# Two graph layers with top-p attention: other slots for logits, exponentials and search passes in step 2, and another order of the closing work on VectorE

## The chip, the cores and the metric

The kernel runs on one core of one Trainium2 chip. The metric is the device time of one execution in microseconds (us); smaller is better. A profiled execution shows what each engine does: TensorE (PE in the profile, with its weight loads as PEld), VectorE (DVE), ScalarE (ACT), GpSimd (POOL) and SyncE (SP, which here only issues DMAs).

## The reference, cut to what matters

There are N = 2708 nodes with D = 256 features. A first layer gives x1 from `adj @ x`. The second layer runs two steps; R below is the row-normalized `adj + I`.

```python
for n in range(2):
    q = Xa @ W1.T @ W2.T;  k = Xa @ W3.T
    probs = softmax(q @ k.T)               # (N, N)
    mask = smallest set of largest probs that reaches 0.9 per row
    A = probs * mask / sum
    Xf = R @ Xf;  Xa = A @ Xa
    Z = Z + Xf @ U1[n].T + Xa @ U2[n].T
h = X + Z
x = layernorm(X + layernorm(h) * g + b)    # two normalizations per row at the end
```

## The kernel before

All matrices are cut into tiles of 128 rows: NB = 22 tiles, of which the last, called EDGE, has 20 rows. The work order is written by hand. An engine executes its instructions in the order in which the program emits them[...], so the place in the program text is the place in each engine's queue.

**Step 2** is the loop `for per in range(NB + 1)`. Each turn is a period, and a period has six groups, g = 0 to 5 (NG = 6). Four tiles are in flight in a period:

- Tile per + 2 (`b_exp`) gets its logits, in three pieces of up to 1024 columns, into one PSUM buffer (`ps_lg`, bufs=1). The PE makes a piece at L506. ScalarE takes the exponential of each piece (`exps2`, L818), and after the first piece also a half-power exponential (L822). The first piece of the tile of the next period is made at g = 5 already. Its row maximum is taken by VectorE in `shift` (L815).
- Tile per + 1 (`b_act`) gets two trials of a threshold on ScalarE in `try_act`, k = 0 and 1: a Relu pass (L922), a Sign pass (L925), and small operations that end in b.u[k] (L936; L938 for k = 1).
- Tile per (`b_dve`) is finished on VectorE: `last_level` (L959 to L962, which needs b.u[1] of the period before), then `finish2`, whose parts are spread over the groups: a masking pass (L976), 20 maxima (L979), sorting (L576, L578), selection among ties (L989 to L1007), and the final mask (L1010). After it comes `begin_search` of tile per + 2 at g = 5 (L826 to L829), which needs all three exponentials.
- Tile per - 1 (`t_mul`) is multiplied on the PE. In each group `turn` makes four transposes (L526, into the PSUM tile tr with two buffers), ScalarE copies them to SBUF (wT, L529), and `products` makes the product one group later (L563).

`r_units` puts the sparse product with R between these on the PE (L730). Its operands are gathered by GpSimd DMAs (L698, yg), and VectorE takes the result in `r_out` (L753 in periods 0 to 10, L768 from period 11). From period 11 finished rows also appear, and `final_slot` normalizes them in stages: at g = 2 it loads x1b, at g = 3 VectorE makes the statistics of up to four tiles (L1037, L1038), at g = 5 ScalarE takes the square roots (L1087), and at g = 0 of the next period VectorE makes reciprocals (L1089, L1090), ScalarE normalizes (L1047) and GpSimd applies g and b (L1062, L1063); at g = 1 finished tiles are stored (L1070). A tile goes through this twice, since there are two normalizations.

In a group the emission order is: on the PE `turn`, then logits, then `r_units`, then `products`; on ScalarE the wT copy, then the exponentials, then the trial passes.

**The closing work** follows the loop. In the last period (per = 22) the EDGE tile's 20 rows are multiplied in one go by `edge_product` (L543, L545, L549), in four row groups which `edge_sum` adds up (a ScalarE copy L240 and a matmul L242). Then come the flags (L1184 to L1197: do the rows stay inside the fast path's assumptions), the arrival of the EDGE tile's sum (L768), and rounds of `final_slot` until all tiles are stored. While the list `tail` is empty, `norm` and `middle` of class Final run on ScalarE and GpSimd; once it isn't, on VectorE (L1045, L1054, L1056).

Of the kernel before, what the change touches and what calls it, by code (L numbers as in the profile page):

```python
# [9 lines left out]
FP = mybir.dt.float32  # L10
I32 = mybir.dt.int32
AF = mybir.ActivationFunctionType
ALU = mybir.AluOpType
# [7 lines left out]
P = 128  # L21
# [127 lines left out]
def fast_path(ctx, tc, c, flags, fint, xT_d, x_d, w0_d, b0_d, w1_d, w2_d, w3_d, u1_d, u2_d, g_d, b_d):  # L149
    nc = tc.nc  # L150
    N, D, DA, NB, DC, KH, CHS, rows = c.N, c.D, c.DA, c.NB, c.DC, c.KH, c.CHS, c.rows
# [8 lines left out]
    small = ctx.enter_context(tc.tile_pool(name="small", bufs=4))  # L160
# [8 lines left out]
    def ps_acc(t=None):  # L169
        acc = ps.tile([P, CH], FP, tag="acc", name="acc")  # L170
        if t == NB - 1:
            nc.vector.memset(acc[:, :D + 1], 0.0)
        return acc

    def ps_misc():
        return ps.tile([P, CH], FP, tag="misc", name="misc")
# [53 lines left out]
    EDGE = NB - 1  # L230
# [5 lines left out]
    def edge_sum(acc, n, stop=True):  # L236

        p = rows(EDGE)
        four = work.tile([P, 4, P], FP, tag="wT", name="four").rearrange("p k i -> p (k i)")
        nc.scalar.copy(four[:, :n], acc[:, :n])  # L240
        whole = ps_acc()
        nc.tensor.matmul(whole[:p, :n], lhsT=fold[:, :p], rhs=four[:, :n], start=True, stop=stop)  # L242
        return whole
# [254 lines left out]
    def logits(s, t, i):  # L498


        p = rows(t)
        lg = ps_lg()
        cs = CHS[2 * i:2 * i + 2]
        for h, (a, b) in enumerate(cs):
            o = slice(DA * h, DA * h + DA)
            nc.tensor.matmul(lg[:p, h, :b - a], lhsT=q[o, t * P:t * P + p], rhs=keys[s][o, i, :b - a],  # L506
                             start=True, stop=True)
        a, b = cs[0][0], cs[-1][1]
        return lg.rearrange("p h n -> p (h n)")[:p, :b - a], a, b
# [7 lines left out]
    NG = (NB + 3) // 4  # L517
# [81 lines left out]
    def exps1(t):  # L599

        p = rows(t)
        e = es[t % 4]
        nmax, srt = st1[t]
        z = small.tile([P, 2], FP, tag="z1", name="z1", bufs=3)
        st1[t] = (srt, z)
        h = 11 * P

        def part(i):
            if i == 0:
                nc.scalar.activation(srt[:p], srt[:p], AF.Exp, bias=nmax[:p], scale=1.0)  # L610
            a, b = ((0, h), (h, N))[i]
            nc.scalar.activation(e[:p, a:b], e[:p, a:b], AF.Exp, bias=nmax[:p], scale=1.0,
                                 accum_out=z[:p, i:i + 1])
        return part
# [76 lines left out]
    later = [[], []]  # L691
    ready = []
# [46 lines left out]
    def za_load(m):  # L739


        if loads.get(m):
            loads[m] = 2
            return None
        loads[m] = 1
        base = work.tile([P, D], FP, tag="in", name="base", bufs=3)
        nc.sync.dma_start(out=base[:rows(m)], in_=za_d[m * P:m * P + rows(m), :])
        return base
# [33 lines left out]
    def e2(t):  # L782
        return es[(t + 2) % 4]
# [30 lines left out]
    def shift(b, lg):  # L814
        nc.vector.tensor_reduce(b.nmax, lg[:, :P], AX.X, ALU.max, negate=True)  # L815

    def exps2(b, i, lg, a, c_):
        nc.scalar.activation(e2(b.t)[:b.p, a:c_], lg, AF.Exp, bias=b.nmax, scale=1.0,  # L818
                             accum_out=b.all[:b.p, i:i + 1])
        if i == 0:  # L820
            nc.scalar.activation(b.half, b.nmax, AF.Identity, bias=part_of[:b.p], scale=0.5)
            nc.scalar.activation(e2(b.t)[:b.p, HC:2 * HC], lg, AF.Exp, bias=b.half, scale=0.5, accum_out=b.roots)  # L822
# [23 lines left out]
    part = exps1(0)  # L846
# [5 lines left out]
    part = exps1(1)  # L852
# [11 lines left out]
    for t in range(NB):  # L864
        acc = ps_acc(t)
        part = exps1(t + 2) if t + 2 < NB else None
        b = None
        if t >= NB - 3:
            b = blocks[t - (NB - 3)] = Block(t - (NB - 3))
        ra_next = finish1(t + 1) if t + 1 < NB else None  # L870
        for g in range(NG):
# [5 lines left out]
            if b and g in (0, 2):  # L877
                lg = logits(1, b.t, g // 2)
# [136 lines left out]
    new, finals, done = [], [], []  # L1015
    tail = []

    mvs = small.tile([P, 4, 2], FP, tag="mvs", name="mvs", bufs=1)
    sds = small.tile([P, 4], FP, tag="sds", name="sds", bufs=1)
    nbs = small.tile([P, 4], FP, tag="nbs", name="nbs", bufs=1)  # L1020
    nc.gpsimd.memset(mvs, 1.0)

    class Final:
# [44 lines left out]
        def store(self):  # L1068
            t, p = self.t, self.p
            nc.sync.dma_start(out=out_d[t * P:t * P + p, :], in_=self.h[:p])  # L1070

    def final_slot(i):


        if i == 2:
            while ready and len(new) < 2:
                new.append(Final(*ready.pop(0)))
                new[-1].load()
        if i == 1:
            while done:  # L1080
                done.pop().store()
        n = len(new) + len(finals)
        if i == 3:
            for k, f in enumerate(new + finals):
                f.stats(k)
        if i == 5 and n:
            nc.scalar.activation(sds[:, :n], mvs[:, :n, 1], AF.Sqrt, bias=c.eps, scale=1.0)  # L1087
        if i == 0 and n:
            nc.vector.reciprocal(sds[:, :n], sds[:, :n])  # L1089
            nc.vector.scalar_tensor_tensor(nbs[:, :n], mvs[:, :n, 0], -1.0, sds[:, :n], op0=ALU.mult, op1=ALU.mult)  # L1090
            for f in finals:
                f.end()
            for f in new:
                f.middle()
            done[:] = finals
            finals[:] = new
            new.clear()

    accs = {}
# [18 lines left out]
    lg = logits(1, 3, 0)  # L1118
    r_units(first - 9)
    try_act(b0, 1, 0)  # L1120
    next_level(b0, 1)
    for per in range(NB + 1):
        n_r = units.get(per, 0)
        b_act = blocks.get(per + 1)
        b_dve = blocks.get(per)
        t_mul = per - 1 if per else None
        if per:
            accs[t_mul] = ps_acc(t_mul)
        masks = None
        b_exp = None  # L1130
        if per and per + 2 < NB:
            b_exp = blocks[per + 2] = Block(per + 2)
        for g in range(NG):
            n = n_r * (g + 1) // NG - n_r * g // NG
            now = later.pop(0)
            later.append([])
            if g == 0:
                if b_exp:
                    shift(b_exp, lg[0])
                r_units(n)  # L1140
            if t_mul == EDGE:
                if g == 0:
                    products(0)
                    edge_product(ya, accs[EDGE], e2(EDGE))
            elif per:
                turn(t_mul, g, ya, accs[t_mul], e2(t_mul))
            if b_exp and g == 3:
                lg = logits(1, b_exp.t, 2)
            if g == NG - 1 and 3 < per + 3 < NB:
                lg = logits(1, per + 3, 0)  # L1150
            if g:
                r_units(n)
            if b_exp and g == 1:
                lg = logits(1, b_exp.t, 1)
            if t_mul != EDGE:
                products(1 if per else 0)
            if b_exp and g in (0, 1, 3):
                exps2(b_exp, (g + 1) // 2, *lg)
            if b_act:
                for k, part in {0: ((0, 0),), 1: ((0, 1), (0, 2), (0, 3)), 2: ((1, 0),), 3: ((1, 1), (1, 2), (1, 3))}.get(g, ()):  # L1160
                    try_act(b_act, k, part)
            if g == 0:
                if b_dve:
                    last_level(b_dve)
                    masks = finish2(b_dve)
                    next(masks)
                final_slot(0)
                if per > 1:

                    t = t_mul - 1  # L1170
                    base = za_load(t)
                    later[0].append(lambda t=t, base=base: arrive(t, base, accs.pop(t), ras.pop(t)[:rows(t)]))
            elif masks:
                next(masks, None)
                if b_exp and g == 5:
                    begin_search(b_exp)
            for f in now:
                f()
            if g:
                final_slot(g)  # L1180
    tail.append(True)


    nc.vector.tensor_scalar(flags[:, 2 * NB:3 * NB], bulk[:, 0, :], 1.0e30, None, op0=ALU.is_ge)  # L1184
# [5 lines left out]
                                   op0=ALU.mult, op1=ALU.is_lt)  # L1190
    nc.vector.tensor_reduce(flags[:, 5 * NB:6 * NB], bulk[:, 5:, :].rearrange("p w t -> p t w"), AX.X, ALU.max)
    nc.vector.tensor_scalar(flags[:, 5 * NB:6 * NB], flags[:, 5 * NB:6 * NB], 8.0, None, op0=ALU.is_ge)
    nc.vector.tensor_reduce(fcol, flags, AX.X, ALU.add)
    accs[EDGE] = edge_sum(accs[EDGE], D)
    pf = ps_misc()
    nc.tensor.matmul(pf[:1, :1], lhsT=fcol, rhs=onec, start=True, stop=True)
    nc.vector.tensor_copy(fint, pf[:1, :1])  # L1197
    t = NB - 1
    base = za_load(t)
    for f in later[0] + later[1]:  # L1200
        f()
    final_slot(0)
    final_slot(1)
    arrive(t, base, accs.pop(t), ras.pop(t)[:rows(t)])
    while ready or finals:
        for g in (2, 3, 5, 0, 1):
            final_slot(g)
    assert not r_queue and len(arrived) == NB

def general_path(ctx, tc, c):  # L1210
# [358 lines left out]
```

## Time and profile before

| | us |
|---|---|
| runs shown, median of 3 | 1396.02 (1394.66 to 1401.23) |
| the profiled execution's own time | 1395.44 |
| its span, first to last instruction | 1393.4 |
| step 2 from period 0's masking pass to the last period | 800.3 to about 1370 |
| one period, periods 2 to 10 | 24.3 to 24.9 |
| one period, periods 16 to 19 | 26.5 to 26.8 |
| last period and closing work | 1370 to 1393.4 |

The own time is 2.0 us above the span, and the median of the runs is 0.6 us above the own time. A period is read as the distance between two starts of L976, which occurs once in each. In step 2 VectorE is busy for nearly the whole period; the PE and ScalarE have pauses in it, and which of the pauses count is the question of the prediction.

### The profile page before, as it was taken

How to read it: one execution, taken by the hardware profiler on the slowest of the kernel's cores; microseconds unless marked ns; L12 is line 12 of the kernel's file. 1: busy time of each engine (PE TensorE's matmuls, PEld its weight loads, DVE VectorE, ACT ScalarE, POOL GpSimd, SP SyncE). 2: the span in 40 equal slices, each digit the busy share in tenths (PEclk: the TensorE clock that was granted, in tenths of full speed). 3: DMA queues.
4: the chain of work that ended last, by engine and by line, in shares of the span. 5: the costliest groups of instructions: out<-in, count | busy, mean ns of one | idle time of the engine just before them, and what ended most of it. 6: DMA issues, size and time to landing. Idle time of an engine off the chain costs nothing.

```text
span 1393.4 us, 18921 instructions
## 1 busy us (share of the span) xinstructions
PE 1279.4 (92%) x5788; PEld 898.7 (64%) x5788; DVE 1044.1 (75%) x3482; ACT 743.9 (53%) x1340; POOL 645.0 (46%) x595
## 2 busy tenths in 40 slices
PE   8999999988999999999998849999998988898884
PEld 6877877833567666666666437777665766566662
DVE  2544545865888887776751379999999988999996
ACT  1000000035455555555554438888887887899951
POOL 1000000014544532775555286776734757677870
PEclk9999999999999999999999879999999999999997
DMA  6544544512222110232223245545432544345351
GB/s 184 179 152 151 164 147 150 165 36 66 67 91 65 52 56 9 88 101 63 65 64 94 84 132 156 159 146 156 138 98 88 158 137 128 114 147 177 123 146 36
DMA packets 92830, 157.94 MB, mean 113 GB/s; under 512 B 16356, under 2 KB 65196, under 8 KB 92720
## 3 DMA queue, kind: packets, MB, share of 16 engines
q1 hardware_dynamic: 66434, 100.59, 22.7%
q0 software_dynamic: 20544, 51.17, 13.1%
q10 hardware_dynamic: 5742, 4.89, 1.3%
q8 instruction: 48, 0.79, 0.2%
q14 instruction: 62, 0.51, 0.1%
HBM read 125.33 MB, written 31.26 MB: 112 GB/s over the span
## 4 chain that ended last, share of the span: by engine, by line
PE 55%; DVE 36%; issue 3%; ACT 3%; another core or an unknown queue 1%; POOL 1%; DMA 0%; ACTq 0%; DVEq 0%; POOLq 0%
PE acc L563 16%; PE acc L255 15%; PE lg L506 6%; DVE cand L979 6%; DVE w L1007 5%; PE tr L526 5%; DVE e L1010 4%; DVE w L976 4%; PE misc L677 3%; DVE srt L576 3%; DVE spare L578 3%; PE acc L649 2%; PE misc L427 2%; PE acc L461 2%; PE misc L422 2%
## 5 line engine op out<-in xcount | busy, mean ns | idle before, releaser
L529 ACT COPY wT<-tr 128x512 f32<-128x512 f32 (+2 forms) x258 | 131.9, 518 | 242.0 <-PE tr L526 158.6
L563 PE MATMUL acc<-ya,wT 128*128 128x256 f32 (+1 forms) x924 | 235.8, 396 | 12.3 <-ACT wT L529 8.8
L563 PE MATMUL acc<-x,wT 128*128 128x256 f32 (+1 forms) x924 | 233.0, 391 | 6.6 <-ACT wT L529 6.6
L698 POOL DMA_INDIRECT yg<-yf_d,ix x154 | 192.6, 1251 | 95.3 <-PE misc L730 50.2
L698 POOL DMA_INDIRECT yg<-v_d,ix x154 | 194.8, 1265 | 85.5 <-PE tr L526 35.2
L563 PEld LDWEIGHTS acc<-x,wT 128*128 128x128 f32 (+1 forms) x924 | 166.5, 191 | 88.0 <-issue 48.5
L563 PEld LDWEIGHTS acc<-ya,wT 128*128 128x128 f32 (+1 forms) x924 | 172.2, 194 | 67.9 <-issue 26.4
L255 PE MATMUL acc<-y,adj_t 128*128 128x257 f32 (+1 forms) x924 | 208.8, 382 | 0.0
L365 POOL DMA_INDIRECT adj_t<-in_adj,ix x154 | 171.8, 1116 | 50.8 <-issue 39.9
L255 PEld LDWEIGHTS acc<-y,adj_t 128*128 128x128 f32 (+1 forms) x924 | 171.7, 189 | 33.8 <-issue 10.2
L730 PE MATMUL misc<-yg,adj_t 128*128 128x256 f32 (+1 forms) x660 | 174.4, 398 | 13.5 <-DVE v L753 7.0
L506 PE MATMUL lg<-k,q 64*128 64x512 f32 (+3 forms) x528 | 152.5, 601 | 26.9 <-ACT e L822 24.4
L526 PE MATMUL tr<-ident,e 128*128 128x128 f32 (+2 forms) x946 | 150.5, 279 | 19.3 <-DVE e L1010 18.9
L730 PEld LDWEIGHTS misc<-yg,adj_t 128*128 128x128 f32 (+1 forms) x660 | 118.5, 193 | 60.1 <-issue 20.7
L526 PEld LDWEIGHTS tr<-ident,e 128*128 128x128 f32 (+2 forms) x946 | 115.3, 142 | 61.8 <-issue 21.4
L332 POOL DMA_DIRECT2D part_d<-e x1 | 0.6, 573 | 294.5 <-DVE e L331 294.5
L569 DVE MAX8 cand<-e 128x8 f32<-128x170 f32 (+1 forms) x352 | 88.1, 319 | 38.5 <-ACT e L513 28.3
L922 ACT ACTIVATE w<-e,st 128x2708 f32<-128x2708 f32 (+1 forms) x43 | 113.5, 2640 | 0.0
L925 ACT ACTIVATE w<-e,st 128x2708 f32<-128x2708 f32 (+1 forms) x42 | 111.0, 2643 | 0.1
L438 ACT COPY x1T<-tr 128x256 f32<-128x256 f32 (+1 forms) x22 | 8.0, 364 | 192.1 <-PE tr L437 192.1
L979 DVE MAX8 cand<-w 128x8 f32<-128x136 f32 (+1 forms) x440 | 93.5, 284 | 0.8
L576 DVE MAX8 srt<-spare 128x8 f32<-128x128 f32 (+3 forms) x264 | 81.3, 308 | 9.1
(230 smaller groups left out, 1791.7 us busy)
## 6 DMA issues: line engine op xcount, KB each, us to landing
adj_t<-in_adj SPq DMA_DIRECT2D x44, 704.0 KB
adj_t<-adjc_d SPq DMA_DIRECT2D x44, 448.0 KB
adjc_d<-adj_t SPq DMA_DIRECT2D x22, 256.0 KB
base<-za_d SPq DMA_DIRECT2D x41, 128.0 KB
adjc_d<-adj_t SPq DMA_DIRECT2D x22, 192.0 KB
xt<-in_x ACTq DMA_DIRECT2D x21, 128.0 KB
x_d<-x SPq DMA_DIRECT2D x21, 128.0 KB
x1b_d<-xb SPq DMA_DIRECT2D x21, 128.0 KB
```

What stands on the lines that cost most here:

```text
L255: nc.tensor.matmul(acc[:p, :n], lhsT=halves[k // KH][:kw, k % KH, :p], rhs=y[:kw, k, :n], start=k == 0, stop=stop and k == NB - 1)
L365: nc.gpsimd.indirect_dma_start(out=a[:CW, i, :], out_offset=None, in_=adj_rows, in_offset=bass.IndirectOffsetOnAxis(ap=ix[:CW, m, i:i + 1] ...
L506: nc.tensor.matmul(lg[:p, h, :b - a], lhsT=q[o, t * P:t * P + p], rhs=keys[s][o, i, :b - a], start=True, stop=True)
L526: nc.tensor.transpose(tr[:kw, k % 4, :p], e[:p, k * P:k * P + kw], ident[:p, :p])
L529: nc.scalar.copy(wT[:, :full, :p], tr[:, :full, :p])
L563: nc.tensor.matmul(acc[:p, :D], lhsT=wT[:kw, k % 4, :p], rhs=y[:kw, k, :], start=k == 0, stop=k == NB - 1)
L576: nc.vector.max(dst[:p, i:i + 8], src[:p])
L698: nc.gpsimd.indirect_dma_start(out=y[:CW, i, :], out_offset=None, in_=rows_d, in_offset=bass.IndirectOffsetOnAxis(ap=ix[:CW, m, i:i + 1], ...
L730: nc.tensor.matmul(acc[:p, :D], lhsT=a[:kw, k, :p], rhs=rhs, start=k == 0, stop=k == CC)
L922: nc.scalar.activation(scr[:b.p, :N], e, AF.Relu, bias=b.nz, scale=b.l[k], accum_out=b.relu)
L925: nc.scalar.activation(scr[:b.p, :N], e, AF.Sign, bias=b.nz, scale=b.l[k], accum_out=b.sign)
L979: nc.vector.max(cand[:p, 8 * i:8 * i + 8], w[:p, SEG2 * i:SEG2 * (i + 1)])
```

## The change

Four things are altered in step 2 and after it.

1. **Logits and exponentials.** The second and third pieces of the logits are made at g = 2 and 4 instead of 1 and 3, the second no longer ahead of the first product. Their exponentials move with them.
2. **Trial passes.** The four parts of `try_act` move one group later: g = 1, 2, 3, 4 instead of 0, 1, 2, 3.
3. **The last period.** `tail` is set as period 22 begins, so its norms and middles run on VectorE; the last `final_slot(5)` is left out.
4. **The closing work.** It is written out. The flags' matmul precedes `edge_sum`; the EDGE tile's statistics, square root and middle come as soon as its sum has arrived, and the ends of the other tiles and the first norm of tile 20 come behind them. mvs, sds and nbs get eight columns.

```diff
+        if per == NB:
+            tail.append(True)
...
-            if b_exp and g == 3:
+            if b_exp and g == 4:
                 lg = logits(1, b_exp.t, 2)
             if g == NG - 1 and 3 < per + 3 < NB:
                 lg = logits(1, per + 3, 0)
             if g:
                 r_units(n)
-            if b_exp and g == 1:
+            if b_exp and g == 2:
                 lg = logits(1, b_exp.t, 1)
             if t_mul != EDGE:
                 products(1 if per else 0)
-            if b_exp and g in (0, 1, 3):
-                exps2(b_exp, (g + 1) // 2, *lg)
+            if b_exp and g in (0, 2, 4):
+                exps2(b_exp, g // 2, *lg)
             if b_act:
-                for k, part in {0: ((0, 0),), 1: ((0, 1), (0, 2), (0, 3)), 2: ((1, 0),), 3: ((1, 1), (1, 2), (1, 3))}.get(g, ()):
+                for k, part in {1: ((0, 0),), 2: ((0, 1), (0, 2), (0, 3)), 3: ((1, 0),), 4: ((1, 1), (1, 2), (1, 3))}.get(g, ()):
                     try_act(b_act, k, part)
...
-            if g:
+            if g and (per < NB or g < NG - 1):
                 final_slot(g)
-    tail.append(True)
+    t = EDGE
+    base = za_load(t)
+    last = Final(t, None)
+    last.load()
+    for f in later[0] + later[1]:
+        f()
...
-    accs[EDGE] = edge_sum(accs[EDGE], D)
     pf = ps_misc()
     nc.tensor.matmul(pf[:1, :1], lhsT=fcol, rhs=onec, start=True, stop=True)
     nc.vector.tensor_copy(fint, pf[:1, :1])
-    t = NB - 1
-    base = za_load(t)
-    for f in later[0] + later[1]:
-        f()
-    final_slot(0)
-    final_slot(1)
+    accs[t] = edge_sum(accs[t], D)
     arrive(t, base, accs.pop(t), ras.pop(t)[:rows(t)])
-    while ready or finals:
-        for g in (2, 3, 5, 0, 1):
-            final_slot(g)
+    _, last.h = ready.pop()
+    n = len(new) + len(finals)
+    last.stats(n)
+    roots(0, n + 1)
+    over(0, n + 1)
+    last.middle()
+    last.stats(5)
+    roots(5, 6)
+    for f in finals:
+        f.end()
+        f.store()
+    for k, f in enumerate(new):
+        f.middle()
+        f.stats(6 + k)
+    over(5, 6)
+    last.end()
+    last.store()
+    roots(6, 6 + len(new))
+    over(6, 6 + len(new))
+    for f in new:
+        f.end()
+        f.store()
```

`roots(a, b)` is the square root on ScalarE for those columns (L1087 before), and `over(a, b)` the reciprocal and the scaled mean on VectorE (L1089, L1090 before).

More of the change, by code (lines that the diff above doesn't have):

```diff
@@ L1016, in fast_path @@
     tail = []
-    mvs = small.tile([P, 4, 2], FP, tag="mvs", name="mvs", bufs=1)
-    sds = small.tile([P, 4], FP, tag="sds", name="sds", bufs=1)
-    nbs = small.tile([P, 4], FP, tag="nbs", name="nbs", bufs=1)
+    mvs = small.tile([P, 8, 2], FP, tag="mvs", name="mvs", bufs=1)
+    sds = small.tile([P, 8], FP, tag="sds", name="sds", bufs=1)
+    nbs = small.tile([P, 8], FP, tag="nbs", name="nbs", bufs=1)
     nc.gpsimd.memset(mvs, 1.0)
@@ L1070, in store, with roots, over @@
             nc.sync.dma_start(out=out_d[t * P:t * P + p, :], in_=self.h[:p])
+    def roots(a, b):
+        nc.scalar.activation(sds[:, a:b], mvs[:, a:b, 1], AF.Sqrt, bias=c.eps, scale=1.0)
+    def over(a, b):
+        nc.vector.reciprocal(sds[:, a:b], sds[:, a:b])
+        nc.vector.scalar_tensor_tensor(nbs[:, a:b], mvs[:, a:b, 0], -1.0, sds[:, a:b], op0=ALU.mult, op1=ALU.mult)
     def final_slot(i):
@@ L1086, in final_slot @@
         if i == 5 and n:
-            nc.scalar.activation(sds[:, :n], mvs[:, :n, 1], AF.Sqrt, bias=c.eps, scale=1.0)
+            roots(0, n)
         if i == 0 and n:
-            nc.vector.reciprocal(sds[:, :n], sds[:, :n])
-            nc.vector.scalar_tensor_tensor(nbs[:, :n], mvs[:, :n, 0], -1.0, sds[:, :n], op0=ALU.mult, op1=ALU.mult)
+            over(0, n)
             for f in finals:
@@ L1178, in fast_path @@
                 f()
-            if g:
+            if g and (per < NB or g < NG - 1):
                 final_slot(g)
-    tail.append(True)
+    t = EDGE
[4 more added lines that the diff above has]
+        f()
+    assert not ready
     nc.vector.tensor_scalar(flags[:, 2 * NB:3 * NB], bulk[:, 0, :], 1.0e30, None, op0=ALU.is_ge)
```

## The prediction

> **What bounds the kernel now.** I read the table of stretches first, then each engine's waits, then the timeline of one late period and of the end. Stretches are start:end, length, busy us (instructions) of PE, PEld, DVE, ACT and POOL, granted clock, DMA. The first is periods 2 to 9, the second periods 15 to 19:
>
> ```profile
> 855.56:1052.11 196.55, 188.76 (x898) 137.59 (x897) 187.98 (x632) 160.75 (x266) 125.94 (x100) 1.00 0.46 137
> 1185.62:1319.33 133.71, 117.02 (x533) 84.68 (x532) 127.81 (x444) 124.23 (x200) 101.57 (x86) 0.96 0.46 144
> ```
>
> VectorE is busy 187.98 of 196.55 us and 127.81 of 133.71 us, which leaves 1.07 and 1.18 us a period, nearly all pauses under 0.1 us between its own dependent instructions. Its waits over 830:1372 confirm it (waiter <- releaser: total, times, longest):
>
> ```profile
> DVE nmax L815 <- PE tr L526: 2.4, 1, 2.4
> DVE part L1004 <- DVE part L1002: 1.7, 3, 0.8
> DVE bulk L999 <- remote: 1.6, 1, 1.6
> ```
>
> In 22 periods VectorE waited for another engine's result once. The 6.3 us at L1010 in period 0 lies upstream of everything changed. Second, the PE's waits from 1186 to 1320, and three instants of the timeline near 1264 (start, us, engine, line):
>
> ```profile
> PE lg L506 <- ACT e L822: 11.8, 5, 4.9
> PE acc L563 <- ACT wT L529: 3.9, 6, 1.3
> ```
> ```profile
> 1263.19 0.29 ACT L936 ACTIVATE st<-st 128x1 f32<-128x1 f32 x1
> 1264.83 0.21 DVE L959 SCALAR_TENSOR_TENSOR st<-st 128x1 f32<-128x1 f32 x1
> 1266.80 0.60 PE L526 MATMUL tr<-ident,e 128*128 128x128 f32 x4
> ```
>
> The PE loses 1.7 us a period waiting until the half-power exponential frees the logits buffer, and starts a period's transposes at 1266.80, 2.85 us after e was ready (1263.95). Yet VectorE doesn't feel it: b.u was ready (1263.48) 1.3 us before L959. These PE pauses are off the path. Last, the end:
>
> ```profile
> 1372.91 5.42 PE L549 MATMUL acc<-ya,wT 128*20 128x256 f32 x44 [0.65 <-ACT wT L545]
> ...
> 1376.04 0.43 DVE L1037 BATCH_NORM_STATS2 bst<-yg 128x6 f32<-128x256 f32 x1 [3.90 <-POOL yg L1063]
> ...
> 1378.87 0.61 PE L242 MATMUL acc<-four,fold 128*20 128x256 f32 x2 [0.54 <-ACT four L240]
> ...
> 1381.96 0.47 DVE L768 SCALAR_TENSOR_TENSOR h<-acc,ra,base 20x256 f32<-20x256 f32 x1
> ...
> 1387.07 0.40 DVE L1045 TENSOR_SCALAR h<-h,sds,nbs 20x256 f32<-20x256 f32 x1
> ```
>
> The EDGE sum is there at 1379.48, but VectorE, held 3.90 and 0.84 us for GpSimd's norms, takes it only at 1381.96.
>
> **What the Trainium skill says.** "Perfetto Trace Analysis", section "Optimization Strategy", says to search for gaps on the engine that binds and that a repeating gap there can mean too few buffers. The repeating 1.7 us is such a buffer gap, but on the PE, not on VectorE. "SBUF — State Buffer", section "Who interferes with whom", says that a VectorE instruction with two SBUF inputs and a GpSimd instruction that reads SBUF exclude each other. The trace fits: gathers at L698 that meet L976 or L1010 take 3.2 to 3.6 us, others 0.95. It is the one link through which shifted gathers could touch VectorE. "ScalarE: Activation LUTs", section "What ACT_TABLE_LOAD costs", gives about 1283 ns; this trace shows 1.28, twice in a late period. The change keeps both.
>
> **Part 1 and 2, the slots.** No instruction is added or removed; VectorE's order in periods 1 to 21 is untouched, and so are the SP and POOL queues there. So I test each result that VectorE awaits, in a late period counted from e ready (0; the next is at 26.8), with durations from the timeline 1262:1294.
>
> ScalarE before: copy, table load, two exponentials, Relu pass, four norms, copy. After: copy 0.58, table 1.28, exponentials with small work 2.5, norms 1.96, second copy 0.5, and only then the Relu pass; so the second copy ends some 2.6 us earlier against its start. The norms may now wait for nbs (VectorE, at 6.15): 0.75 us. Total work stays 25.1 us and starts at about 1.15, and b.u[1], now behind the fourth copy (+0.5 us), is ready at 25.2; L959 reads it at 27.65. The reserve is 2.4 us (before 1.3), because the start comes earlier.
>
> PE: tr0 at 0.1, then product, tr1, r, product reach 4.7 without the 1.7 us wait; a wait of 1.5 for the second copy and 0.6 for the fourth follow. At g = 5 a new wait: the next tile's first logits need the single buffer, now freed by the third exponential at 21.3 while the PE arrives at 19.6, so 1.7 us. Behind it stand r (1.0) and a product (1.8); it ends at 25.4, r of the next period brings it to 26.3, and tr0 starts on time, 2.7 us earlier than before. The logits are there at 22.4; L815 needs them at 27.5. The 1.7 us pause has moved, not gone, and the lateness is gone. In periods 1 to 10 the same table gives the PE finished at 23.0 of 24.45 and b.u at 21.4 of 25.3. The gathers: the PE needs the second chain at 11.5 instead of 16.6; its first gathers are issued from -2.4 and the seventh ends at 10.9, wanted at 22. Covered.
>
> Value: 0 for 20 periods. If that cover fell, ScalarE's next delay of 2.4 us or the PE's of 0.5 plus VectorE's 2.4 would be felt first. The 2.42 us wait of period 14 (logits that VectorE got late) lies between 0 (its cause is outside) and -2.42 (logits 2.7 us earlier swallow it). The trace doesn't show the cause: I take half, **-1.2**. Shifted gathers meeting VectorE: the unexplained waits L1004, L999, L1007, L994 sum to 4.1 us over 830:1372; value 0, between -4.1 (all vanish) and +4.1 (as many again).
>
> **Part 3 and 4, the end.** On VectorE from 1370.35, start-to-start steps from the trace: reciprocal and nbs 0.36; two norms (L1045) 0.65; two middles, each 0.51 + 0.41, 1.84; two L768 0.90; three statistics 1.62 (0.53 to 0.56 each); flags 1.56. That is 1377.3; added against before are the four middle instructions and two norms, removed are the waits 3.90 and 0.84. The flags' matmul waits behind L549, which ends at 1378.33 (released by L545, nothing changed ahead), so fint is done by 1378.85. The EDGE sum comes at 1379.48 as before, and L768 starts at **1379.53** instead of 1381.96: 2.43 earlier. SP: the EDGE row store now follows VectorE's middles, at 1373.7 instead of 1371.10; the same kind of store to reload took 1.7 us (1365.47 to 1367.17), so the reload goes at 1375.4 and, at an estimated 2 us more, lands 2 us before it is needed. The x1b load moves before the last stores; its buffer is free at 1373.2.
>
> After arrival: L768 0.50, statistics 0.64, root 0.36, over 0.38, middle 1.01, statistics 0.55, two ends 0.69, tile 20's middle 1.02 and statistics 0.55, over 0.40, end 0.36, over 0.40, end 0.41: 7.27, so 1386.8. Before it was 5.51 to 1387.47: tile 20's work was already done on the way. So of 2.43 us, 1.76 is given back: **-0.7**. The final store and what follows keep their 5.9 us. If GpSimd's norms were no cover, i.e. the reload came late, the part gives 0; with every step 10% shorter, -1.4.
>
> **Sum.** -1.2 - 0.7 = -1.9 against the profiled execution's 1395.44 (span 1393.4 and 2.0 around it): 1393.5. The median of the runs is 0.6 higher: **1394.1**. Its own bounds: -0.7 - 2.4 - 4.1 and +4.1 around 1396.0, so 1388.8 to 1400.1. A measurement of this kernel can tell about 0.5%, 7 us, from no change.
>
> **Rivals.**
> - *A new ring binds (slower).* Copy, exponentials, passes, third exponential, then logits at g = 5, r, product, r, tr0, copy form one ring through the single logits buffer. Summed without waits it is 19.3 on ScalarE and 5.5 on the PE, 24.8 of 26.8. It decides from 2.0 us of further waits a period. At 3 us it costs 1.0 in each of the nine periods 11 to 19: about 1404.3. For it: the two waits for copies are already inside the ring. Against it: they are 2.1 at most, and the first doesn't reach ScalarE. With clashes at the shared port it could come as well: 0.5 us in 20 periods is +10, 1405. Together 0.12.
> - *The late PE was what set 26.8 (faster).* The PE's own round was 26.65 (1155.24 to 1181.89), suspiciously near. If VectorE's 1.18 us of pauses were hidden waits, nine periods give 8 us: 1387.3. Against: periods 2 to 9, where the PE waits for VectorE, have pauses of 1.07 too. 0.09.
> - *Nothing moves.* The reload or another late step eats the end's gain and period 14's wait stays: 1396.0. 0.15.
>
> The likeliest case has 0.64. With "nothing moves" it makes 0.79 within 0.5%; faster 0.09, slower 0.12. The range, 1389 to 1401, reaches a little into the slower case.
>
> **What would show it.** Right: periods 2 to 10 at 24.5 and 16 to 19 at 26.8; the PE's wait L506 <- L822 gone, one at L506 for L818 of about 1.7 in its place, and a wait of the PE for L1010 in late periods; L768 of EDGE at about 9.6 us after L1012 instead of 12.0; the last L1045 0.7 earlier. Wrong: a VectorE wait at L826, L815 or L959 repeating each period, or late periods below 26.3.

## The result, and the profile after

The changed kernel takes 1404.89 us (median of 20 runs, 1398.72 to 1411.99) against 1397.86 us of the kernel before in the same comparison (20 runs). The ratio is 1.0051, with a 95% interval of 1.0036 to 1.0067: slower by 7 us, above the predicted range. The profiled execution's own time is 1409.25 us and its span 1407.5 us, that is 14.1 us more span than before. The two medians differ by half of that, so the profile shows a costly instance of what the runs pay.

The 14.1 us were added up from the starts of L976. Step 2 begins 2.0 us later (nothing was changed ahead of it), period 0 takes 1.4 us more, periods 1 to 14 together 0.0, periods 15 to 19 **11.7**, the way from there to the EDGE tile's L1012 0.1, and the end 1.0 less. So the loss sits in the late periods. The same two stretches after (start:end, length, busy us of PE, PEld, DVE, ACT, POOL, granted clock, DMA):

```profile
858.95:1056.83 197.88, 186.26 (x885) 135.58 (x884) 187.71 (x633) 162.17 (x266) 123.31 (x99) 1.00 0.46 134
1189.01:1334.38 145.37, 126.10 (x543) 91.51 (x540) 128.33 (x445) 124.30 (x199) 88.89 (x89) 0.91 0.43 135
```

VectorE's work in periods 15 to 19 is the same (127.81 us before, 128.33 after) and ScalarE's as well; only the length has grown. It has become waiting. The granted clock, lower here (0.91 against 0.96), is not the cause: in period 15 it was 1.00 from 1189.01 to 1213.65, that is through the whole of the first long wait below, and 0.54 only in the 10.5 us from 1216.00 on. VectorE's waits of that stretch, where before there was none above 0.3 us (waiter <- releaser: total, times, longest):

```profile
DVE e L1010 <- remote: 5.3, 2, 3.0
DVE nmax L815 <- PE misc L730: 3.2, 1, 3.2
DVE st L959 <- ACT st L938: 2.4, 2, 1.4
```

L959 and L815 are places that the prediction named as signs of its being wrong. L1010 is stranger: what it waits for is a semaphore of VectorE itself. (The label "remote" stands where the update that ended a wait has no instruction in the profile that ended shortly before it.) The timeline of period 15 (start, us, engine, line; in brackets the idle time before it) shows it:

```profile
1206.08 0.38 PE L526 MATMUL tr<-ident,e 128*128 128x128 f32 x2
...
1209.95 0.71 DVE L1007 MATCH_REPLACE8 w<-part,e 128x544 f32<-128x544 f32 x1
...
1211.81 0.95 POOL L698 DMA_INDIRECT yg<-v_d,ix  x1 [0.31 <-issue]
...
1213.65 3.05 DVE L1010 SCALAR_TENSOR_TENSOR e<-w,st,e 128x2720 f32<-128x2720 f32 x1 [3.00 <-remote]
1215.16 0.27 ACT L529 COPY wT<-tr 128x128 f32<-128x128 f32 x1 [3.17 <-remote]
...
1215.50 2.02 POOL L698 DMA_INDIRECT yg<-v_d,ix  x1 [2.75 <-remote]
```

L1010 needs what L1007 left at 1210.66 and starts at 1213.65. ScalarE's copy needs the transposes that ended at 1206.46 and starts at 1215.16, 8.7 us later, though ScalarE was free from 1211.99. GpSimd pauses too. All three move again within 2.8 us after the last of an unbroken row of gathers (0.95 us each, 0.30 apart) ended at 1212.76. The trace's record of semaphore updates has the same picture: none of the PE's between 1203.75 and 1215.07 and then ten within 0.43 us, and VectorE's own one, which frees L1010, at 1213.63. Ten is also the number of the PE's instructions that raise its semaphore and ended between 1206.25 and 1213.38. (The record leaves out updates in this trace, as shown under the experiments, so an absence alone would prove nothing.) The operands were ready and the signals of it came late. The Trainium skill, "Perfetto Trace Analysis", section "Summary: the profiler window per engine type", lists the propagation of semaphores among what the profile hides for VectorE, ScalarE and TensorE alike; this is where such a delay would be. Here it is 3.0 us for VectorE and between 3.2 and 8.7 us for ScalarE.

Why is there a row at that moment? The gathers of L698 stand behind GpSimd's four norm operations, and these wait for ScalarE's norms (L1047). Before the change, in period 15 (which starts at 1185.62):

```profile
1191.80 2.63 ACT L922 ACTIVATE w<-e,st 128x2708 f32<-128x2708 f32 x1
...
1194.42 1.08 ACT L1047 ACTIVATE yg<-yg,nbs,sds 128x256 f32<-128x256 f32 x2
...
1199.25 0.99 POOL L698 DMA_INDIRECT yg<-v_d,ix  x1
...
1207.28 3.05 DVE L1010 SCALAR_TENSOR_TENSOR e<-w,st,e 128x2720 f32<-128x2720 f32 x1
```

After it, in the same period (start 1189.01):

```profile
1193.17 1.09 ACT L1047 ACTIVATE yg<-yg,nbs,sds 128x256 f32<-128x256 f32 x2
...
1195.62 2.65 ACT L922 ACTIVATE w<-e,st 128x2708 f32<-128x2708 f32 x1
...
1198.02 0.99 POOL L698 DMA_INDIRECT yg<-v_d,ix  x1 [0.15 <-issue]
```

With the Relu pass one slot later, the norms stand ahead of it on ScalarE. The gathers start 9.0 us into the period instead of 13.6, while L1010's turn comes at 21.6 in both. So 11 gathers are issued ahead of it instead of 7.

The end came as worked out. EDGE's L1012, the matmul of `edge_sum`, L768 and the last L1045:

```profile
1385.10 0.15 DVE L1012 RECIPROCAL ra<-bulk 20x1 f32<-20x1 f32 x1
...
1393.67 0.15 DVE L1210 CAST fint<-misc 1x1 int32<-1x1 f32 x1 [1.24 <-PE misc L1209]
...
1394.62 0.47 DVE L768 SCALAR_TENSOR_TENSOR h<-acc,ra,base 20x256 f32<-20x256 f32 x1 [0.81 <-PE acc L242]
...
1401.23 0.41 DVE L1045 TENSOR_SCALAR h<-h,sds,nbs 128x256 f32<-128x256 f32 x1
```

L768 comes 9.5 us after L1012 (predicted 9.6) and now waits for the PE's sum. The last L1045 comes 16.13 us after L1012 instead of 17.12: 1.0 earlier, predicted 0.7.

### The profile page after: what moved, and what is told of

It reads as the page before. It is cut to its first block, busy times and chain, and to the rows that moved or that the text cites. A ratio compares the mean times of both kernels' runs of the same rounds, so it can differ in the third digit from the quotient of the medians.

```text
span 1407.5 us, 18878 instructions
## 1 busy us (share of the span) xinstructions
PE 1285.6 (91%) x5788; PEld 904.5 (64%) x5788; DVE 1046.6 (74%) x3488; ACT 744.5 (53%) x1336; POOL 620.3 (44%) x591
## 4 chain that ended last, share of the span: by engine, by line
PE 55%; DVE 32%; ACT 7%; issue 3%; another core or an unknown queue 2%; DMA 0%; ACTq 0%; DVEq 0%
PE acc L563 16%; PE acc L255 15%; PE lg L506 6%; DVE cand L979 5%; DVE w L1007 4%; PE tr L526 4%; DVE w L976 4%; DVE e L1010 4%; PE misc L677 3%; DVE srt L576 3%; DVE spare L578 3%; PE acc L649 2%; PE misc L427 2%; PE misc L390 2%
## 5 line engine op out<-in xcount | busy, mean ns | idle before, releaser
L698 POOL DMA_INDIRECT yg<-yf_d,ix x154 | 191.0, 1240 | 96.7 <-PE misc L730 40.0
L698 POOL DMA_INDIRECT yg<-v_d,ix x154 | 175.8, 1141 | 103.0 <-PE tr L526 40.7
L730 PE MATMUL misc<-yg,adj_t 128*128 128x256 f32 (+1 forms) x660 | 179.3, 407 | 16.2 <-remote 8.3
L506 PE MATMUL lg<-k,q 64*128 64x512 f32 (+3 forms) x528 | 151.8, 603 | 31.1 <-ACT e L818 15.8
```

The costliest lines, as they stand in the source:

```text
L698: nc.gpsimd.indirect_dma_start(out=y[:CW, i, :], out_offset=None, in_=rows_d, in_offset=bass.IndirectOffsetOnAxis(ap=ix[:CW, m, i:i + 1], ...
L730: nc.tensor.matmul(acc[:p, :D], lhsT=a[:kw, k, :p], rhs=rhs, start=k == 0, stop=k == CC)
```

## The experiments

Three theories were carried through. **L**: signals come late behind long rows of gathers. **R**: the ring through the single logits buffer binds. **P**: GpSimd and VectorE exclude each other more often.

One thing has to be known first. In these comparisons the kernel before itself took either about 1374 us or about 1400 us, always compared within one session. Below they are called *A sessions* (1397.86 for the first result; later 1403.27, 1402.03, 1398.28) and *B sessions* (1374.32, 1373.55). The number of the chip doesn't decide it: number 2 gave 1373.55 once and 1402.03 another time.

The traces tell the sessions apart as well, by their record of semaphore updates. The table sets the updates recorded for VectorE's semaphore, from the first L976 on, beside VectorE's instructions there that raise it:

| kernel (session) | updates recorded | instructions |
|---|---|---|
| before (A) | 713 | 1028 |
| changed (A) | 615 | 1029 |
| after_late (A), experiment 5 | 672 | 1023 |
| after_plain (A), experiment 2, without the gathers | 1031 | 1029 |
| slots_only (B), experiment 1 | 1029 | 1028 |

In the first 300 us, where no gather is issued yet, every trace has one update for each instruction. So in A sessions, and only there, updates are missing where gathers are issued. Whether they were merged or only not recorded is not shown.

**1. The parts alone (a B session, 1374.32).** `tail_only` has parts 3 and 4, `slots_only` parts 1 and 2. `logits_only` and `passes_only` are part 1 and part 2 alone:

```diff
 # logits_only
-            if b_exp and g == 3:
+            if b_exp and g == 4:
                 lg = logits(1, b_exp.t, 2)
...
-            if b_exp and g == 1:
+            if b_exp and g == 2:
                 lg = logits(1, b_exp.t, 1)
...
-            if b_exp and g in (0, 1, 3):
-                exps2(b_exp, (g + 1) // 2, *lg)
+            if b_exp and g in (0, 2, 4):
+                exps2(b_exp, g // 2, *lg)
 # passes_only
-                for k, part in {0: ((0, 0),), 1: ((0, 1), (0, 2), (0, 3)), 2: ((1, 0),), 3: ((1, 1), (1, 2), (1, 3))}.get(g, ()):
+                for k, part in {1: ((0, 0),), 2: ((0, 1), (0, 2), (0, 3)), 3: ((1, 0),), 4: ((1, 1), (1, 2), (1, 3))}.get(g, ()):
```

> The kernel before with parts 3 and 4 alone (the end on VectorE, written out), the slots of step 2 as before. Three theories of the loss: (L) late signals: while GpSimd issues many gathers in a row, semaphore signals between the other engines arrive late, and the slots put a longer row ahead of L1010; (R) ring: the single logits buffer, freed one group later, makes ScalarE and the PE late; (P) port: L1010 and a gather exclude each other at the shared SBUF port. All three put the loss into the slots, so here: L768 of the EDGE tile about 9.6 us after L1012 instead of 12.0, the end 0.7 us earlier, waits of VectorE in periods 11 to 21 as before (below 3 us in all), time 1397.2. If the end costs time, 1398 to 1402.

> The kernel before with parts 1 and 2 alone (logits, exponentials and trial passes in the later slots), the old end. All three theories: the whole loss, 1405 to 1406, with VectorE waiting 8 to 15 us in periods 11 to 21 at L1010, L959 and L815. If the end is the cause: 1398.

> Only the logits' second and third piece and their exponentials move (g = 2 and 4); the trial passes stay. R: the whole loss, +6 to +8 us, with waits at L959 and L815 and the PE's wait L506 for L818. L: the PE comes earlier and with it the gathers, but the Relu pass stays ahead of the norms, so GpSimd's norms stay where they were; the row ahead of L1010 grows less: 0 to +4 us. P: about +3 us at L1010 alone.

> Only the trial passes move one group later; logits and exponentials stay. R: no loss (0), since the logits buffer is freed as early as before. L: the PE still waits for the half-power exponential, so the gathers stay late and the row ahead of L1010 stays near 7 to 9: 0 to +2 us. P: 0 to +3 us by chance of the gathers' place.

Measured: tail_only 1371.61 us, ratio 0.9984 [0.9975, 0.9992]; slots_only 1372.35, 0.9984 [0.9973, 0.9995]; passes_only 1371.75, 0.9986 [0.9974, 0.9999]; logits_only 1423.27, 1.0347 [1.0322, 1.0371]. The slots that lost in the first result lose nothing here. Periods 15 to 19 of slots_only:

```profile
1165.99:1299.81 133.82, 116.32 (x543) 83.84 (x541) 127.92 (x445) 124.10 (x200) 102.70 (x90) 0.99 0.47 148
```

26.76 us a period, as predicted, although here too 11 gathers stand ahead of L1010 in every one of them. So a long row delays nothing in a B session. tail_only, which has the kernel before's step 2, takes 27.06 us in each of the periods 14 to 18: its VectorE instruction L1004 takes 0.49 us there, in slots_only 0.24 to 0.25. So the slots gain about 0.25 us in each of these periods of a B session; what lengthens L1004 was not tried. The PE's waits over 1166:1300 are those that the prediction named:

```profile
PE lg L506 <- ACT e L818: 6.8, 4, 1.7
...
PE tr L526 <- DVE e L1010: 5.2, 5, 3.4
```

The ring is real, though: with the logits moved and the passes left, it binds. VectorE's waits of logits_only from 790 us on:

```profile
DVE bulk L826 <- ACT e L818: 19.5, 16, 2.6
DVE bst L1037 <- POOL yg L1063: 16.5, 15, 4.1
DVE nmax L815 <- PE lg L506: 13.1, 16, 1.5
```

That is R's sign, in 16 periods. The whole change shows no such row, which speaks against R; it also shows why the passes had to move together with the logits.

**2. The whole again, its slots, and two edits of the gathers (an A session, 1403.27).** `after_again` is the changed kernel, `slots_again` is slots_only. In `after_break` the second chain's gathers get work ahead of them; in `after_plain` a plain transfer stands in their place, which leaves the gather out (R's product gets wrong rows):

```diff
 # after_break, in y_load
+        for _ in range(10 if s == 1 else 0):
+            nc.gpsimd.memset(idle, 0.0)
 # after_plain, in y_load
-        for i in range(CC):
-            nc.gpsimd.indirect_dma_start(out=y[:CW, i, :], ...)
+        nc.sync.dma_start(out=y[:CW, :CC, :], in_=rows_d[:CW * CC, :].rearrange("(c p) d -> p c d", p=CW))
```

> The whole change once more, on a chip that may not be the one of the first result. Three theories. L: the loss of the first result is VectorE waiting at L1010 and L959 for signals that come late behind a long unbroken row of GpSimd's gathers; then it appears where such waits appear: with them about +7 us (ratio near 1.005), without them the sum of the two parts as measured apart, about -4 us (0.997). R: a ring through the single logits buffer costs about 1 us in each late period: ratio 1.005 on any chip, with VectorE waits at L826 or L815 in each period. P: VectorE and GpSimd exclude each other more often: 1.005 on any chip, with longer L976 and L1010 and no waits.

> The slots of step 2 alone, the end as before. L: like the whole change plus 2 us: 1.006 on a chip with late signals, 0.998 on one without. R and P: 1.006 on any chip.

> The whole change, with ten GpSimd memsets of 128x112 ahead of the seven gathers of each second chain (s = 1), so that two loads' gathers no longer form one row. L: the waits of VectorE at L1010 fall to under 0.5 us, and the time falls to that of the slots without late signals (ratio 0.997 to 0.999 where the whole change has 1.005; no difference where it has 0.997). R: no change against the whole change. P: no change or slower by some us, since GpSimd has more work that writes SBUF.

> The whole change, with the seven indirect gathers of each load in y_load replaced by one plain transfer on SP's queue; this leaves out the gather (R's product gets wrong rows). L: no waits with late signals at all, period 0 falls by the 6.3 us of its wait where that exists; ratio 0.992 to 0.998. R: the ring has no gather in it: as slow as the whole change, but for period 0. P: all clashes of gathers with L976 and L1010 vanish: some 20 x 0.3 to 0.5 us, 6 to 10 us, on any chip.

Measured: after_again 1411.83, 1.0071 [1.0044, 1.0098]; slots_again 1415.32, 1.0101 [1.0073, 1.0130]; after_break 1430.56, 1.0199 [1.0172, 1.0225]; after_plain 1378.42, 0.9822 [0.9796, 0.9847]. The loss is back and it belongs to the slots. Without L698's gathers it is gone, and 25 us more with it (1378.42 against 1403.27): the gathers delay the kernel before as well.

The break's time missed what L said. Its waits at L1010, L959 and L815 are gone in the late periods, but another took their place. VectorE's waits of after_break over 1120:1400 (the lines of this kernel stand four higher, L1041 is L1037):

```profile
DVE bst L1041 <- POOL yg L1067: 26.1, 14, 3.6
DVE bst L1041 <- issue: 6.5, 2, 3.2
```

GpSimd's memsets and the gathers behind them made its norms late for VectorE's statistics. The edit changed two things at once and decides nothing by its time.

**3. Fewer gathers (a B session, 1373.55).** `before_plain` is the kernel before with after_plain's edit. `after_half` is the changed kernel with four gathers and one plain transfer of the other three chunks. `tail_again` and `passes_again` repeat two parts.

> The kernel before, with the seven indirect gathers of each load replaced by one plain transfer on SP's queue; this leaves out the gather (R's product gets wrong rows). The changed kernel without gathers measured 0.982 of the kernel before. L: the change's loss sits in the gathers alone, so without them both kernels are nearly alike: this one 0 to 4 us slower than the changed one without gathers, by the end's gain and the slots' small gain; ratio 0.982 to 0.986 on a chip with late signals, 0.994 to 1.000 on one without. R or P with another cause in the slots: this one is faster than the changed one without gathers by the 7 to 10 us that the change costs, ratio 0.975 on a chip with late signals.

> The whole change, with three of the seven gathers of each load replaced by one plain transfer (leaves out these three chunks' gather); the rows of gathers become 8 instead of 14. L: the waits at L1010, L959 and L815 in late periods fall from 1 to 3 us to under 0.5 and period 0's 6.3 us to under 1: within 4 us of the kernel without any gather, ratio 0.980 to 0.987 on a chip with late signals. If the delay is a sum over gathers instead of a matter of long rows, half of the loss stays: ratio near 0.993. On a chip without late signals 0.992 to 0.998 either way.

> The order of the last period alone, the slots of step 2 as before. The prediction's step gives -0.7 us, 0.9995; the first run on another chip gave 0.9984. L: step 2 as before, so nothing of the loss: 0.997 to 1.000 on any chip.

> The search passes of ScalarE one slot later, logits and exponentials as before. L: the loss comes from the PE reaching its second chain of R's product earlier, which starts the gathers earlier; the passes alone don't move the PE's order, so at most a third of the loss of the slots: 0.998 to 1.003 on a chip with late signals. If the passes' order on ScalarE is what makes VectorE late: 1.007 to 1.010 there. On a chip without late signals 0.9986 again.

Measured: before_plain 1371.19, 0.9977 [0.9964, 0.9990]; after_half 1370.86, 0.9976 [0.9965, 0.9986]; tail_again 1371.54, 0.9988 [0.9979, 0.9997]; passes_again 1372.11, 0.9985 [0.9974, 0.9997]. Taking the gathers away from the kernel before gains 2.4 us here. These four can't tell L from the others, since nothing loses; experiment 4 asks the same where it does.

**4. The same questions in an A session (1402.03).** `after_third` is the changed kernel; the other three are before_plain, passes_only and after_half again.

> The whole change a third time. So far it cost 7 and 9 us where the kernel before takes about 1400 us, and its parts alone gained 2 us each where that takes about 1374 us; the whole was not yet timed on a chip of the second kind. There the sum of the parts says -3.5 us: ratio 0.9975, with late periods of 26.8 and no wait of VectorE at L1010, L959 or L815. A ring (R) or clashes (P) that only the whole change shows would give 1.002 or more there. On a chip of the first kind again 1.005 to 1.010.

> The kernel before without the gathers (one plain transfer for seven gathers; leaves the gather out). On a chip of the first kind, if the gathers carry the change's whole loss (L): 0 to 4 us slower than the changed kernel without gathers, which had 0.982 there, so 0.982 to 0.986, and its late periods at 26.8. If the slots lose something else as well on such a chip: 0.975. On a chip of the second kind 0.9977 as before.

> ScalarE's search passes one slot later, alone. On a chip of the first kind: 0.998 to 1.003 if the loss comes with the PE's new order (its chains of R's product and so the gathers start earlier), 1.007 to 1.010 if it comes with ScalarE's. On a chip of the second kind 0.9985 as before.

> The whole change with three of seven gathers of each load made one plain transfer (leaves these chunks' gather out). On a chip of the first kind: 0.980 to 0.987 and no VectorE wait over 0.5 us in late periods if only long rows of gathers delay; about 0.993 if the delay adds up over gathers. On a chip of the second kind 0.9976 as before.

Measured: after_third 1412.51, 1.0079 [1.0054, 1.0105]; before_plain2 1377.69, 0.9835 [0.9813, 0.9858]; passes_third 1409.93, 1.0060 [1.0037, 1.0082]; after_half2 1376.44, 0.9829 [0.9806, 0.9851]. Without L698's gathers the two kernels are alike in A sessions too (0.9822 and 0.9835, each against the kernel before of its own session), so the change's whole loss needs the gathers. With them go also 24.3 us of the kernel before itself, ten times as much as in the B session. Four gathers a load instead of seven, in rows of eight instead of fourteen, already take it all away, with no wait of VectorE above 0.4 us left. So the loss is not in proportion to the number of gathers. after_half2 also keeps the changed order of the PE and of ScalarE, so that order alone doesn't make the loss. Periods 15 to 19 of before_plain2 and of after_plain:

```profile
1164.66:1298.30 133.64, 117.87 (x547) 83.36 (x545) 127.74 (x444) 123.98 (x201) 14.37 (x20) 1.00 0.46 148
```
```profile
1171.56:1305.17 133.61, 117.62 (x543) 85.06 (x541) 127.70 (x444) 123.94 (x200) 14.40 (x20) 0.98 0.46 148
```

passes_third fell between the two values expected of it, nearer to ScalarE's order as the cause. The PE's order is the old one there, and still 7.9 of the whole change's 10.5 us appear. Its VectorE waits over 1177:1330 are mostly for ScalarE, at L959, and not at L1010:

```profile
DVE st L959 <- ACT st L935: 3.8, 2, 2.1
DVE st L959 <- ACT st L938: 2.9, 3, 1.9
DVE st L959 <- ACT st L928: 2.1, 1, 2.1
DVE e L1010 <- DVE w L1007: 1.0, 1, 1.0
```

This corrected L: not the PE's new order starts the gathers earlier, as the expectation had it, but ScalarE's norms, which stand ahead of the Relu pass in both versions.

**5. The norms put back (an A session, 1398.28).** `after_late` is the changed kernel with final_slot(0) one slot later, so that ScalarE does the Relu pass first and then the norms, as before. VectorE's two small operations ahead of the norms (reciprocal and scaled mean) and the stage after them move along. The orders on the PE and on GpSimd in step 2 are those of the changed kernel, instruction by instruction in the traces. `tail_third` is tail_only.

```diff
-                final_slot(0)
...
-            if g and (per < NB or g < NG - 1):
-                final_slot(g)
+            for i in {0: (), 1: (0,), 2: (1, 2)}.get(g, (g,)):
+                if per < NB or i < NG - 1:
+                    final_slot(i)
```

> The whole change, with ScalarE's four norms of a period put back behind the first search pass, as they stand in the kernel before (final_slot(0) one slot later; logits, exponentials, passes and the end stay as changed). GpSimd's own norms then start about 10 us into a late period instead of 5.8, and its row of 14 gathers about 11 us ahead of L1010's turn instead of 14. Theory L in its last form (the earlier start of the row is what brings the delay): where the kernel before takes about 1400 us, the waits at L1010, L959 and L815 fall under 0.5 us a period and the ratio to 0.996 to 1.001 instead of 1.007; where it takes 1374 us, 0.9970 to 0.9985. If instead the PE's new order or ScalarE's shorter slack brings the loss: 1.005 to 1.010 again in the first case.

> The order of the last period alone. Step 2 is as before, so on a chip of either kind the end's part shows by itself: the prediction said -0.7 us (0.9995); 0.9984 and 0.9988 were measured where the kernel before takes 1374 us. Expected where it takes 1400 us: 0.997 to 1.000; slower than 1.001 would mean that the end as well pays for late signals.

Measured: after_late 1394.23, **0.9977 [0.9965, 0.9989]**; tail_third 1396.81, 1.0000 [0.9986, 1.0014]. Putting the norms back turns 1.005 to 1.008 into a gain of 4 us. Not all of that gain lies in the late periods: from the EDGE tile's L1012 to the end its trace takes 21.2 us, the changed kernel's 22.4 and the kernel before's 23.4; why this end is shorter still was not tried. Periods 15 to 19 of after_late, and then the first gather behind the norms and L1010 in its period 18, which starts at 1263.4: 13.6 and 21.6 us into it, as before the change.

```profile
1182.92:1316.70 133.78, 119.11 (x548) 86.01 (x546) 127.89 (x444) 124.77 (x201) 105.46 (x91) 0.98 0.49 149
```
```profile
1276.98 0.99 POOL L698 DMA_INDIRECT yg<-v_d,ix  x1
```
```profile
1285.03 3.05 DVE L1010 SCALAR_TENSOR_TENSOR e<-w,st,e 128x2720 f32<-128x2720 f32 x1
```

The gathers counted between the norms and L1010's turn in periods 14 to 19, and VectorE's waits of 0.3 us and more in these periods, from the traces:

| kernel (session) | gathers ahead of L1010 | waits of VectorE, us a period |
|---|---|---|
| before (A) | 9, 7, 7, 7, 7, 7 | 2.4, 0, 0, 0, 0, 0 |
| changed (A) | 11, 11, 9, 9, 11, 9 | 1.5, 3.0, 1.4, 3.2, 2.3, 1.1 |
| after_again (A) | 11, 9, 8, 11, 9, 9 | 3.1, 1.3, 3.5, 3.1, 1.4, 0 |
| after_third (A) | 9, 8, 10, 10, 9, 8 | 1.4, 1.9, 2.1, 2.9, 1.6, 1.4 |
| slots_again (A) | 10, 9, 8, 10, 11, 9 | 1.7, 0.8, 0.4, 1.2, 3.1, 0.3 |
| passes_third (A) | 9, 9, 9, 9, 9, 9 | 0.5, 1.7, 1.5, 2.1, 2.1, 1.9 |
| after_late (A) | 7, 8, 9, 7, 7, 8 | 0, 0, 0, 0, 0, 0 |
| slots_only (B) | 11 in each | 0 in each |

In these A rows 11 gathers always went with a wait of 1.5 us or more, 7 never with one (period 20 of the changed kernel, outside the table, had 11 and no wait). At 8 or 9 it goes either way, so the count is not the whole condition; what else belongs to it is not shown. The place of the row depends on the session too: tail_only, with the kernel before's step 2 in a B session, starts it 10.7 us into the period with 9 gathers ahead of L1010. P falls as the cause of the loss: L976 and L1010 took 67.1 to 67.2 us each for all 22 periods, before, after, in slots_only and in after_late alike, and all of VectorE's work in periods 15 to 19 grew by only 0.5 us of the 11.7.

**What stays open.** Why signals come late behind gathers in one session and not in another, and by which path, no run here shows; nor whether the lateness and the missing updates have one cause, or whether the recording itself has a part in it. after_half2 is without the loss though 259 of its 1029 updates are missing. That L959's and L815's waits come from ScalarE's late copies is read from the timelines, not tried apart. The whole change and after_late were not timed in a B session; the sum of the parts, -2.7 and -2.0 us against 1374.32, is an estimate for the first.

## Why the prediction was wrong, point by point

- **Slots, "value: 0 for 20 periods": the step that failed.** Its list of what VectorE awaits was right as far as it went. In a B session its late period holds to the digit: 26.76 us, with the PE's wait at L506 for L818 of 1.7 us in the place of the old one (though tail_only takes 27.06 there, so that the slots gain a little). What it left out is that the Relu pass moving behind the norms lets *GpSimd* start earlier. The prediction wrote that the SP and POOL queues are untouched and priced the gathers as "covered". Their order is untouched; their time isn't. It asked when the gathered rows are needed and never what else happens while they are issued. The term of the sum should have been about +8 us for the first result (7.0 measured, and the 1.0 that the end gives back) instead of 0; slots_again measured it alone at 12. In the profile 11.7 us of it lie in periods 15 to 19, as waits of VectorE at L1010, L815 and L959.
- **"Contention, between -4.1 and +4.1".** The right kind of term with the wrong link and size. Following the Trainium skill, "SBUF — State Buffer", section "Who interferes with whom", the prediction let gathers touch VectorE only by excluding one another. That would lengthen instructions; measured, L976 and L1010 kept their 3.05 us, and VectorE lost 10.9 us in five periods by waiting. (Gathers that start during one of the two take 2.5 to 3.6 us over the kernel before's step 2; the prediction's 3.2 to 3.6 is the range of its late window.)
- **Signs that were set aside.** The 6.3 us at L1010 in period 0 was put aside as lying upstream. It looks like the same event: it is labelled "remote", a row of 18 gathers runs across it (804.47 to 826.69, with L1010 starting at 826.95), and in slots_only and after_plain it is gone. The 2.42 us of period 14 was taken at half, "the cause isn't shown"; tail_third, with the same step 2, has 2.4 us at L815 labelled "remote", in period 15, and the B sessions have none. That period 14 is 1.1 us shorter after the change, near the -1.2, is luck: it now has a wait of 1.5 us at L1010 in place of the 2.4 at L815, and periods 1 to 14 together gained 0.0.
- **The end, -0.7: right in the profile**, where it is 1.0 us. tail_only, tail_again and tail_third have 0.9984, 0.9988 and 1.0000, that is 2.7, 2.0 and 1.5 us in the medians, the last not told from zero by its interval. The first two exceed even the prediction's -1.4. In the B traces the last L1045 comes 16.1 us after L1012 in tail_only and tail_again, 16.5 to 16.8 in slots_only, passes_only and passes_again, so the end itself explains 0.3 to 0.7 us of them; the rest stays open.
- **The rivals.** The ring (slower, 1404.3 us) gave nearly the measured number by the wrong mechanism: L815 and L826 don't wait in each period. logits_only shows the ring when it does bind, at 1.0347. "The late PE sets 26.8" falls: the PE is on time in slots_only, and the periods stay at 26.76. (Nine times 1.18 us would be 10.6, not the 8 put down for it.)

## What to carry to other kernels

When an operation moves on one engine, follow everything that it lets go earlier or later on the others, to the end of the chain: here Relu pass, norms, GpSimd's norms, gathers. "Same order" is not "same time". A wait labelled "remote", or for the engine's own semaphore, whose producer has long ended, is worth a look at what GpSimd issues at that moment, and one such wait in a trace is a warning for every place to which the same kind of row may be moved. Count the recorded semaphore updates against the instructions that make them: here it told one kind of session from the other in every trace with gathers. When a result of half a per cent surprises, time the kernel in a second session before building on it.

## What the runs showed of the hardware

- The same kernel before takes 1374 or about 1400 us, by the session. 24.3 us, set beside the 28.5 between 1373.55 and 1402.03, go away with the 308 gathers of L698 (before_plain2, 1377.69), while in a B session the same edit gains 2.4.
- In the changed kernel's trace (A) work of VectorE and ScalarE started up to 3.0 (6.3 in period 0) and 8.7 us after its producer's end while gathers were issued one after another (0.95 us, 0.30 apart); in B sessions rows as long, of the same durations, left L1010 a wait of 0.04 us and ScalarE's copies at most 0.09 us behind their transposes from period 1 on (slots_only, tail_again).
- From the first L976 on, the record of semaphore updates holds 60 to 75% of VectorE's updates in each A trace with gathers of L698 (615 of 1029 in the changed kernel, 770 of 1029 in after_half2), and all of them in each B trace and in the two A traces without these gathers (after_plain, before_plain2).
